# Two state-space heads rewritten: folded normalization, DMA borders, and a convolution shared by three engines

## The chip, the cores and the metric

The kernel runs on one core of a Trainium2 chip. The core has a matrix engine (TensorE, PE in the profile), a vector engine (VectorE, DVE), an activation engine (ScalarE, ACT), a general engine (GpSimd, POOL) and a queue engine (SyncE, SP), which here only issues DMAs. Each engine works through its own instruction stream in order, and semaphores tie the streams together. The metric is device time in microseconds for one launch, and lower is better. The kernel before takes 1484.87 us, the median of three runs (1484.46 to 1489.54).

## The reference, cut to what matters

Two layers run one after the other on an image of 64 x 64 tokens with 96 channels. All data is fp32. Both layers have this form (the second has its own weights for each of four scan directions, snake orders instead of plain ones, and a true recurrence):

```
xz = norm(x) @ in_proj_w               # 96 -> 384: x_val (192 channels) and z (192)
x_val = silu(depthwise_conv3x3(x_val) + conv_b)
y = sum over 4 scan directions of selective_scan(x_val) + D * x_val
out = (layernorm(y) * silu(z)) @ out_proj_w
```

In the kernel, each layer's input is first normalized over groups of three channels and all tokens; one mean and one variance per group give a factor `rs` and an offset `shift = -mean * rs` for each of the 96 channels. The output of layer 0, added to its input, is the input of layer 1.

## The kernel before

**Layout.** The input of a layer lies as `xT`, 96 channels by 4096 tokens. The 192 inner channels are three blocks `b` of 64 channels. A block's tile has 128 partitions: the lower 64 hold its channels for the first 512 tokens of every chunk of 1024, the upper 64 for the second 512. There are four chunks `c` (`NCH`), and a 512-token piece is 8 image rows (`SR`) of 64 (`HW`). `u[b]` is the result of the convolution, `y[b]` the running sum of the scans, both 128 x 2048.

**Order of a layer.** `head` makes `u`, starts `y` as `D * u`, and writes `silu(z)` to DRAM (`szd`). Then come the scans: in layer 0 `near_scans`, which works only on the ends of the sequences, and a branch that is skipped when it covers everything; in layer 1 `scans`, the long stage from some 256 us to the end. Then a tail applies the layer norm, the gate from `szd` and the output projection.

**The head.** Statistics (L1270 to L1282) end in `shift`. Eight instructions, four on VectorE and four on ScalarE (L1288, L1290), write the normalized input `xn`. `project(b, c)` is two products of 64 columns, one for each half of the partitions, and a ScalarE copy of the result into `pad[b]`, a tile of four chunks of 10 x 66 with room for a border on each side. `borders(b)` computes the row above and the row below each 8-row piece again, by four small products (L1315) and four ScalarE copies (L1319).

The convolution has nine taps. On VectorE, `conv` sums over two chunks at a time (128 x 1052 elements an instruction, L1373 for the first tap and L1375 for the other eight) into an SBUF tile `acc`; it does both pairs of blocks 0 and 1, and the last chunk of block 2. TensorE does three chunks of block 2 (`conv_by_products`, L1350): each tap is a product with a diagonal matrix `diag`, summed in PSUM. ScalarE applies SiLU (L1340) and starts `y` (L1250, `start_y`). Last, `gate(b, c)` takes two products of 64 columns (L1327) and a SiLU (L1332), and a DMA of 128 partitions to `szd` (L1333). PSUM in the head: three rooms for `z`, three for projections and products, two for borders.

**Order of work.** In the head before, engine calls are made on `nc.vector`, `nc.scalar` and so on: the framework's scheduler is free to reorder what is independent, and it moves weight loads of layer 1 into idle places of the SP queue. Calls made on `pe`, `act`, `dve`, `pool` and `sp` keep the order in which they are written on their engine; `near_scans` and `scans` use these. Helpers of this kind give one line number to all they record (L261 in `near_scans`, L738 in `scans`), so tiles' names must tell operations apart.

**What waits for the head.** In layer 0, `near_scans` begins with TensorE products of `u[T]` (tile `nu`), which ScalarE and VectorE copy out (`nus`), and then `npj`, `npd` and so on; `npd` needs the tile `nxd`, set to one by a GpSimd memset (L284). In layer 1, `scans` begins with TensorE's `pj`, twelve instructions over the last chunk of all three `u`; then ScalarE's `xd`, TensorE's `pd` and a softplus on ScalarE and VectorE; then DMAs of `su` to `du` issued by GpSimd.

Of the kernel before, what the change touches and what calls it, by code (L numbers as in the profile page):

```python
# [9 lines left out]
F32 = mybir.dt.float32  # L10
BF16 = mybir.dt.bfloat16
AF = mybir.ActivationFunctionType
ALU = mybir.AluOpType
# [4 lines left out]
HW = 64  # L18
L = HW * HW
# [25 lines left out]
def two_ss2d_layers(  # L45
# [1203 lines left out]
    def start_y(mul, ds, T, s=slice(0, L // 2)):  # L1249
        mul(y[T][:, s], u[T][:, s], ds[:, T : T + 1])  # L1250

    def head(l, xT, w):

        ipw_s, v, ds = w["ipw"], w["v"], w["ds"]
        with ExitStack() as sc:
            cv = sc.enter_context(tc.tile_pool(name=f"cv{l}", bufs=1, reuse_waits="tile"))
            cw = sc.enter_context(tc.tile_pool(name=f"cw{l}", bufs=3, reuse_waits="tile"))
            cvp = sc.enter_context(tc.tile_pool(name=f"cvp{l}", bufs=2, space=PSUM, reuse_waits="tile"))

            pad = [cv.tile([128, NCH, SR + 2, HW + 2], F32, name=f"pad{l}_{b}") for b in range(3)]  # L1260
            for t in pad:
                nc.gpsimd.memset(t[:, :, :, 0:1], 0.0)
                nc.gpsimd.memset(t[:, :, :, HW + 1 : HW + 2], 0.0)
                nc.gpsimd.memset(t[HALF[0], 0, 0, 1 : HW + 1], 0.0)
                nc.gpsimd.memset(t[HALF[1], NCH - 1, SR + 1, 1 : HW + 1], 0.0)


            gst = cv.tile([DM, 7], F32, name=f"gst{l}")
            gm, rs, shift = gst[:, 2:3], gst[:, 5:6], gst[:, 6:7]
            nc.vector.bn_aggr(gst[:, 0:2], w["st"].rearrange("p a b -> p (a b)"))  # L1270
            pm = cvp.tile([DM, 1], F32, tag="z", name=f"pm{l}", bufs=3)
            nc.tensor.matmul(pm, gav, gst[:, 0:1], start=True, stop=True)
            nc.vector.tensor_copy(gm, pm)
            nc.vector.tensor_sub(gst[:, 3:4], gst[:, 0:1], gm)
            nc.vector.tensor_mul(gst[:, 3:4], gst[:, 3:4], gst[:, 3:4])
            nc.vector.tensor_add(gst[:, 4:5], gst[:, 3:4], gst[:, 1:2])
            pv = cvp.tile([DM, 1], F32, tag="z", name=f"pv{l}", bufs=3)
            nc.tensor.matmul(pv, gav, gst[:, 4:5], start=True, stop=True)
            nc.scalar.activation(rs, pv, AF.Ln, bias=eps5[0:DM])
            nc.scalar.activation(rs, rs, AF.Exp, scale=-0.5)  # L1280

            nc.vector.scalar_tensor_tensor(shift, gm, -1.0, rs, ALU.mult, ALU.mult)  # L1282

            xn = cv.tile([DM, L], F32, name=f"xn{l}")
            for g in range(8):
                s = slice(g * 512, (g + 1) * 512)
                if g % 2 == 0:
                    nc.vector.tensor_scalar(xn[:, s], xT[:, s], gm, rs, ALU.subtract, ALU.mult)  # L1288
                else:
                    nc.scalar.activation(xn[:, s], xT[:, s], AF.Identity, bias=shift, scale=rs)  # L1290
            xr = xn.rearrange("p (r w) -> p r w", w=HW)

            def project(b, c):
                ps = cvp.tile([128, HT], F32, tag="in", name=f"in{l}_{b}_{c}", bufs=3)
                for h, half in enumerate(HALF):
                    g = 2 * c + h
                    nc.tensor.matmul(
                        ps[half], ipw_s[:, 64 * b : 64 * b + 64], xn[:, g * 512 : (g + 1) * 512],
                        start=True, stop=True,
                    )  # L1300
                nc.scalar.copy(
                    pad[b][:, c, 1 : SR + 1, 1 : HW + 1], ps.rearrange("p (r w) -> p r w", w=HW)
                )

            def borders(b):

                ps = cvp.tile([128, 2, NCH, HW], F32, tag="ed", name=f"ed{l}_{b}")
                lhs = ipw_s[:, 64 * b : 64 * b + 64]
                for h, half in enumerate(HALF):
                    for below in range(2):  # L1310

                        row = [SR * (2 * c + h + below) - 1 + below for c in range(NCH)]
                        cs = [c for c in range(NCH) if 0 <= row[c] < HW]
                        s = slice(cs[0], cs[-1] + 1)
                        nc.tensor.matmul(  # L1315
                            ps[half, below, s], lhs, xr[:, row[cs[0]] : row[cs[-1]] + 1 : 2 * SR],
                            start=True, stop=True,
                        )
                        nc.scalar.copy(  # L1319
                            pad[b][half, s, (SR + 1) * below, 1 : HW + 1], ps[half, below, s]  # L1320
                        )

            def gate(b, c):
                ps = cvp.tile([128, HT], F32, tag="z", name=f"z{l}_{b}_{c}", bufs=3)
                for h, half in enumerate(HALF):
                    g = 2 * c + h
                    nc.tensor.matmul(  # L1327
                        ps[half], ipw_s[:, DI + 64 * b : DI + 64 * b + 64],
                        xn[:, g * 512 : (g + 1) * 512], start=True, stop=True,
                    )  # L1330
                sz = cw.tile([128, HT], F32, tag="sz", name=f"sz{l}_{b}_{c}")
                nc.scalar.activation(sz, ps, AF.Silu)  # L1332
                nc.sync.dma_start(out=szd[l][b, :, HT * c : HT * (c + 1)], in_=sz)  # L1333

            taps = [(i, j) for i in range(3) for j in range(3)]

            W2 = HW + 2

            def finish(b, cut, of):
                nc.scalar.activation(  # L1340
                    u[b][:, cut].rearrange("p (c r w) -> p c r w", r=SR, w=HW), of, AF.Silu,
                    bias=v[:, b, V_CB : V_CB + 1],
                )
                start_y(nc.scalar.mul, ds, b, cut)

            def conv_by_products(b, c):

                ps = cvp.tile([128, HT], F32, tag="in", name=f"cp{l}_{b}_{c}", bufs=3)
                for k, (i, j) in enumerate(taps):
                    nc.tensor.matmul(  # L1350
                        ps.rearrange("p (r w) -> p r w", w=HW), diag[:, k, :],
                        pad[b][:, c, i : i + SR, j : j + HW],
                        start=(k == 0), stop=(k == len(taps) - 1),
                    )
                finish(
                    b, slice(HT * c, HT * (c + 1)), ps.rearrange("p (c r w) -> p c r w", c=1, w=HW)
                )

            def conv(b, s):


                n = s.stop - s.start
                room = cw.tile([128, 2, SR, W2], F32, tag="acc", name=f"acc{l}_{b}_{s.start}")
                room = room[:, 0:n]
                acc = room.rearrange("p c r w -> p c (r w)")[:, :, 0 : SR * W2 - 2]
                for k, (i, j) in enumerate(taps):
                    o = i * W2 + j
                    src = pad[b].rearrange("p c r w -> p c (r w)")[
                        :, s, o : o + SR * W2 - 2
                    ]  # L1370
                    wk = v[:, b, V_CW + k : V_CW + k + 1]
                    if k == 0:
                        nc.vector.tensor_scalar_mul(acc, src, wk)  # L1373
                    else:
                        nc.vector.scalar_tensor_tensor(acc, src, wk, acc, ALU.mult, ALU.add)  # L1375
                finish(b, slice(HT * s.start, HT * s.stop), room[:, :, :, 0:HW])

            for b in (0, 1, 2):
                project(b, 0)
                project(b, 1)  # L1380
                borders(b)
            for b in (2, 0, 1):
                project(b, 2)
                project(b, 3)
            diag = cv.tile([128, len(taps), 128], F32, name=f"diag{l}")
            for k in range(len(taps)):
                nc.scalar.mul(diag[:, k, :], ident, v[:, 2, V_CW + k : V_CW + k + 1])
            conv(0, slice(0, 2))
            for c in range(NCH - 1):
                conv_by_products(2, c)  # L1390
            for b, c in ((1, 0), (0, 2), (1, 2)):
                conv(b, slice(c, c + 2))
            conv(2, slice(NCH - 1, NCH))
            for b in range(3):
                for c in range(NCH):
                    gate(b, c)

    def tail(l, w, xT):

# [349 lines left out]
```

## Time and profile before

| | us |
|---|---|
| median of three runs | 1484.87 |
| the profiled execution, own time | 1483.21 |
| its span, first to last instruction | 1481.1 |
| head of layer 0: `shift` ready, to first copy of `nus` | 21.32 to 80.36 |
| head of layer 1: `shift` ready, to end of `pj` | 196.47 to 261.61 |
| convolution on VectorE, layer 1, first tap to last | 206.36 to 255.25 |

Busy shares over the span: PE 83%, DVE 91%, ACT 82%, POOL 75%. The span is nearly all `scans` (from 290 us on). In the two heads POOL is idle but for a few memsets.

How to read the rows: a row of the timeline has a start, a length, the engine, the line and operation, the output and input tiles, partitions x elements, a count, and in brackets the idle time before with the instruction that ended it. A group's row ends in busy time and mean ns of one. In the table of stretches each engine has its busy time and number of instructions; the number after POOL's is the clock that TensorE was granted (1.00 is full), then the DMA share and GB/s. TensorE's fp32 products are two instructions each in this profile.

### The profile page before, as it was taken

The page shows a single profiled execution, that of the slowest core. Times are in us where ns is not written, and L with a number is a line of the kernel's source. Part 1 is how long each engine was busy: PE and PEld are TensorE (multiplying, and loading weights), DVE is VectorE, ACT ScalarE, POOL GpSimd, SP SyncE. Part 2 cuts the span into 40 slices and gives each one's busy share as a digit, 9 for nine tenths or more (in the row PEclk, how much of TensorE's full clock was granted, in tenths as well). Part 3 has the DMA queues.
Part 4 walks back from the last instruction along what each step waited for, and adds up shares of the span by engine and source line. Part 5 has one row for each costly group of instructions (what it writes and reads, how often), then busy time and mean ns, then how long its engine had stood idle before and what let it go on. Part 6 is the DMA issues. An engine that isn't in the chain of part 4 may idle for free.

```text
span 1481.1 us, 17275 instructions
## 1 busy us (share of the span) xinstructions
PE 1229.0 (83%) x5091; PEld 487.2 (33%) x5091; DVE 1345.5 (91%) x945; ACT 1212.4 (82%) x2500; POOL 1109.5 (75%) x603
## 2 busy tenths in 40 slices
PE   6955888698788888879888888888889898887898
PEld 3333333233232323233333333333333332322333
DVE  5957679589999999999999999999998999999996
ACT  6564345689999989998999999999997989897873
POOL 1003000379999998989898989898989898989895
PEclk9965889589999999999999999999998999999999
DMA  4230612515262626262626262626262626262634
GB/s 113 74 94 6 154 28 86 129 33 129 70 144 59 148 67 148 58 155 57 145 57 145 59 143 59 143 59 143 60 144 57 143 59 153 61 145 69 144 87 127
DMA packets 79793, 146.30 MB, mean 99 GB/s; under 512 B 27676, under 2 KB 30940, under 8 KB 79596
## 3 DMA queue, kind: packets, MB, share of 16 engines
q1 hardware_dynamic: 78012, 142.58, 39.7%
q0 software_dynamic: 576, 1.57, 0.4%
q10 hardware_dynamic: 1104, 0.98, 0.2%
q8 instruction: 41, 0.67, 0.2%
q14 instruction: 60, 0.49, 0.1%
HBM read 80.85 MB, written 12.13 MB: 63 GB/s over the span
## 4 chain that ended last, share of the span: by engine, by line
DVE 27%; issue 20%; ACT 12%; PE 11%; POOL 10%; DMA 6%; SPq 3%; DVEq 0%; POOLq 0%; ACTq 0%
DVE h L738 15%; DVE b L738 7%; POOL hc L738 7%; ACT a L738 4%; ACT bT L738 3%; DMA cb<-C 3%; PE pj L738 3%; SPq L738 3%; PE ys L738 3%; DVE acc L1375 3%; PE b L738 2%; DMA xT<-xs 2%; POOL sp L738 1%; POOL ln L738 1%; DMA du<-su 1%
## 5 line engine op out<-in xcount | busy, mean ns | idle before, releaser
L738 POOL TENSOR_TENSOR hc<-h,cb 128x1024 f32<-128x1024 f32 x384 | 902.8, 2372 | 92.9 <-DVE h L738 40.1
L738 DVE TENSOR_TENSOR_SCAN h<-a,carry,b 128x1024 f32<-128x1024 f32 x288 | 664.5, 2337 | 23.6 <-PE b L738 2.6
L738 ACT ACTIVATE a<-dt,am 128x1024 f32<-128x1024 f32 x384 | 437.9, 1141 | 56.7 <-DVE h L738 50.6
L738 PE MATMUL ys<-hc,fold 128*64 128x512 f32 x1536 | 430.3, 640 | 0.1
L738 ACT ACTIVATE bT<-duT,BT 128x192 f32<-128x192 f32 x1012 | 386.6, 445 | 2.2
L738 PE MATMUL b<-ident,bT 128*128 128x128 f32 x1536 | 224.1, 289 | 28.9 <-DVE h L738 19.4
L738 DVE TENSOR_TENSOR b<-b,du 128x1024 f32<-128x1024 f32 x192 | 232.0, 1208 | 8.6 <-PE b L738 8.4
L738 PEld LDWEIGHTS b<-ident,bT 128*128 128x128 f32 x1536 | 176.5, 146 | 153.5 <-DVE h L738 90.1
L738 DVE TENSOR_TENSOR_SCAN h<-a,b 128x1024 f32<-128x1024 f32 x96 | 216.4, 2278 | 11.2 <-PE b L738 2.4
L738 PE MATMUL b<-B,selh 96*128 96x512 bf16 x384 | 117.6, 388 | 125.9 <-DVE h L738 125.5
L738 PEld LDWEIGHTS ys<-hc,fold 128*64 128x64 f32 x1536 | 77.7, 138 | 140.0 <-issue 106.3
L738 PEld LDWEIGHTS <-selh 96*128 96x128 bf16 x384 | 25.7, 98 | 255.3 <-DVE h L738 204.9
L738 PE MATMUL pj<-u,xw 64*124 64x512 f32 x192 | 100.6, 671 | 4.3 <-ACT sz L1332 2.0
L1375 DVE SCALAR_TENSOR_TENSOR acc<-pad,v,acc 128x1052 f32<-128x1052 f32 (+1 forms) x80 | 91.4, 1200 | 0.7
L738 POOL DMA_DIRECT2D du<-su x12 | 6.4, 538 | 83.2 <-ACT am L235 80.8
L261 POOL MEMSET nna<- 128x4 f32 (+1 forms) x9 | 1.0, 117 | 86.1 <-ACT nna L261 86.1
L738 ACT CAST B<-pj 96x512 bf16<-96x512 f32 (+2 forms) x96 | 54.9, 575 | 5.1 <-PE pj L738 5.1
L738 POOL TENSOR_TENSOR sp<-sp,ln 128x512 f32<-128x512 f32 x45 | 57.7, 1283 | 0.2
L738 POOL TENSOR_TENSOR ln<-ln,w 128x512 f32<-128x512 f32 x45 | 57.8, 1285 | 0.0
L738 POOL TENSOR_TENSOR su<-sp,u 128x512 f32<-128x512 f32 x45 | 57.6, 1281 | 0.0
L738 PE MATMUL ys<-y,ident 128*128 128x512 f32 (+1 forms) x120 | 57.2, 577 | 0.0
L738 PEld LDWEIGHTS pj<-u,xw 64*124 64x124 f32 x192 | 35.2, 199 | 65.8 <-issue 48.7
(189 smaller groups left out, 1224.0 us busy)
## 6 DMA issues: line engine op xcount, KB each, us to landing
cb<-C SPq DMA_DIRECT2D x256, 256.0 KB
dt<-sp SPq DMA_DIRECT2D x192, 128.0 KB
du<-su SPq DMA_DIRECT2D x180, 128.0 KB
szd<-sz SPq DMA_DIRECT2D x24, 256.0 KB
szt<-szd SPq DMA_DIRECT2D x24, 256.0 KB
xT<-xs SPq DMA_DIRECT2D x8, 384.0 KB
xs<-xT SPq DMA_DIRECT2D x1, 1536.0 KB
xs<-xT SPq DMA_DIRECT2D x8, 192.0 KB
```

What stands on the lines that cost most here:

```text
L261: return lambda *args, **more: tc.keep_in_program_order(op(*args, **more))
L738: return lambda *args, **more: tc.keep_in_program_order(op(*args, **more))
L1375: nc.vector.scalar_tensor_tensor(acc, src, wk, acc, ALU.mult, ALU.add)
```

## The change

It rewrites `head` for both layers.

- The normalization is folded into the projection: VectorE scales the weights by `rs` (`ws`, three instructions), nine products with one moving column (`offset`) give the constant term of every output channel, and one copy makes them a bias tile. `xn` and its eight instructions go; all products read `xT`. The copies into `pad` and the gates' SiLUs add the bias.
- The border rows are no longer computed: after the four copies of a block, four DMAs on SP move rows between the halves of `pad` (64 partitions, rows of 64 elements).
- The convolution is split over more engines. VectorE does three pairs (block 0 both, block 1 the first), with its sums in PSUM (`accs`, five banks). TensorE does three chunks of block 2 as before. Three chunks (block 2's last, block 1's last two) are made by ScalarE, which multiplies each tap into a tile, and GpSimd, which adds the tiles up.
- For blocks 0 and 1, a gate product has all 128 columns and one 512-token piece (`gate01`), and its result goes to `szd` by two DMAs of 64 partitions. Block 2 stays as it was (`gate2`).
- `start_y` moves from ScalarE to GpSimd, six instructions of 128 x 1024, after the convolution.
- All of it is put into a list with times and issued in the order of these times, on the ordered engines. PSUM has three rooms for all other results. The ring of `sz` tiles has four buffers instead of three.

```diff
+            for k in range(9):
+                act.mul(diag[:, k, :], ident, v[:, 2, V_CW + k : V_CW + k + 1])
 ...
+            accs = cvp.tile([128, 5 * HT], F32, name=f"accs{l}")
+            small = accs[:, 4 * SR * W2 : 4 * SR * W2 + 8]
 ...
-            xn = cv.tile([DM, L], F32, name=f"xn{l}")
-            for g in range(8):
-                s = slice(g * 512, (g + 1) * 512)
-                if g % 2 == 0:
-                    nc.vector.tensor_scalar(xn[:, s], xT[:, s], gm, rs, ALU.subtract, ALU.mult)
-                else:
-                    nc.scalar.activation(xn[:, s], xT[:, s], AF.Identity, bias=shift, scale=rs)
+            for cut in (slice(0, 64), slice(64, DI), slice(DI, 2 * DI)):
+                dve.tensor_scalar_mul(ws[:, cut], ipw_s[:, cut], rs)
+            def offset(to, of, n):
+                pe.matmul(
+                    small[to, 2 + n : 3 + n], ipw_s[:, of : of + to.stop - to.start], shift,
+                    start=True, stop=True,
+                )
+            for half in HALF:
+                offset(half, 0, 0)
+            for n in (1, 2):
+                for half in HALF:
+                    offset(half, 64 * n, n)
+            offset(slice(0, 128), DI, 3)
+            for half in HALF:
+                offset(half, DI + 128, 4)
+            dve.tensor_copy(bias, small[:, 2:7])
+            def room(name):
+                return cvp.tile([128, HT], F32, tag="in", name=name, bufs=3)
+            def padded(b, c):
+                act.activation(
+                    pad[b][:, c, 1 : SR + 1, 1 : HW + 1],
+                    live.pop(("in", b, c)).rearrange("p (r w) -> p r w", w=HW),
+                    AF.Identity, bias=bias[:, b : b + 1],
+                )
             def borders(b):
-                ps = cvp.tile([128, 2, NCH, HW], F32, tag="ed", name=f"ed{l}_{b}")
 ...
+                t, n = pad[b], NCH - 1
+                row = slice(1, HW + 1)
+                h0, h1 = HALF
+                sp.dma_start(out=t[h1, :, 0, row], in_=t[h0, :, SR, row])
+                sp.dma_start(out=t[h0, 1:, 0, row], in_=t[h1, :n, SR, row])
+                sp.dma_start(out=t[h0, :, SR + 1, row], in_=t[h1, :, 1, row])
+                sp.dma_start(out=t[h1, :n, SR + 1, row], in_=t[h0, 1:, 1, row])
+            def gate01(g):
+                ps = live["z", g] = room(f"z{l}_{g}")
+                pe.matmul(
+                    ps, ws[:, DI : DI + 128], xT[:, g * 512 : (g + 1) * 512], start=True, stop=True
+                )
+            def gated01(g):
+                c, h = divmod(g, 2)
+                sz = cw.tile([128, HT], F32, tag="sz", name=f"sz{l}_{g}")
+                act.activation(sz, live.pop(("z", g)), AF.Silu, bias=bias[:, 3:4])
+                for b, half in enumerate(HALF):
+                    sp.dma_start(
+                        out=szd[l][b, HALF[h], HT * c : HT * (c + 1)], in_=sz[half]
+                    )
 ...
+            taps = [(i, j) for i in (1, 0, 2) for j in range(3)]
 ...
+            def tap_dve(n, b, c, k):
+                i, j = taps[k]
+                o = i * W2 + j
+                acc = accs[:, 2 * SR * W2 * (n % 2) :][:, 0 : 2 * SR * W2]
+                live["acc", b, c] = acc.rearrange("p (c r w) -> p c r w", r=SR, w=W2)
+                acc = acc.rearrange("p (c t) -> p c t", c=2)[:, :, 0 : SR * W2 - 2]
 ...
+            def tap_act(b, c, k):
+                t = cw.tile(
+                    [128, HT], F32, tag="tap" if k else "sum", name=f"tap{l}_{b}_{c}_{k}",
+                    bufs=3 if k else 2,
+                )
+                live["tap" if k else "sum", b, c, k] = t
+                act.mul(t.rearrange("p (r w) -> p r w", w=HW), source(b, c, *taps[k]), weight(b, *taps[k]))
+            def tap_pool(b, c, k):
+                acc = live["sum", b, c, 0]
+                pool.tensor_add(acc, acc, live.pop(("tap", b, c, k)))
+            t = 0.0
+            for b, order in ((0, (2, 3, 1, 0)), (2, (3, 2, 1, 0)), (1, (3, 2, 1, 0))):
+                for c in order:
+                    at(t, project, b, c)
+                    at(t + 0.95, padded, b, c)
+                    t += 0.9
+                at(t + 1.0, borders, b)
+            for c in range(3):
+                for k in range(9):
+                    at(t + 0.9 * k, tap_pe, 2, c, k)
+                t += 8.1
+                at(t + 0.1, silu, 2, slice(HT * c, HT * (c + 1)), partial(whole, ("cp", c)))
+            for g in range(8):
+                at(t, gate01, g)
+                at(t + 0.5, gated01, g)
+                t += 0.5
+            for c in range(NCH):
+                at(t, gate2, c)
+                at(t + 0.9, gated2, c)
+                t += 0.9
+            t = 2.6
+            for n, (b, c) in enumerate(((0, 2), (0, 0), (1, 0))):
+                for k in range(9):
+                    at(t, tap_dve, n, b, c, k)
+                    t += 1.3
 ...
+            t = 7.4
+            for b, c in ((2, 3), (1, 3), (1, 2)):
+                for k in range(9):
+                    at(t - 1.5, tap_act, b, c, k)
+                    if k:
+                        at(t, tap_pool, b, c, k)
+                        t += 1.3
 ...
+            for n, (b, c) in enumerate(((2, 2), (0, 2), (1, 2), (2, 0), (0, 0), (1, 0))):
+                at(
+                    t + 1.5 + 2.5 * n, start_y, pool.tensor_scalar_mul, ds, b,
+                    slice(HT * c, HT * (c + 2)),
+                )
+            for _, _, step in sorted(steps, key=lambda at: at[:2]):
+                step()
```

## The prediction

> **What bounds the kernel now.** I read the page first, then the chain of waits, then the timeline of each engine in the two heads, since the change touches nothing else. The chain from 193 to 264 us belongs to layer 1:
>
> ```profile
> 196.47 0.47 DVE xn L1288
> ...
> 209.16 12.31 DVE acc L1375 x11
> ...
> 254.49 0.78 DVE acc L1375
> 255.29 0.73 ACT u L1340
> 256.06 5.55 PE pj L738 x8
> ```
>
> VectorE's convolution holds the path from 206.36 to 255.3; then a SiLU, then `pj`. The chain does not reach back into layer 0, so there I read the timeline:
>
> ```profile
> 62.33 9.66 PE L1327 MATMUL z<-xn,ipw 96*64 96x512 f32 x44
> 72.41 1.08 PE L1327 MATMUL z<-xn,ipw 96*64 96x512 f32 x4 [0.42 <-ACT sz L1332]
> 76.98 5.43 PE L261 MATMUL nu<-u,wide 128*128 128x192 f32 x24 [3.49 <-ACT sz L1332]
> 78.97 0.72 ACT L1340 ACTIVATE u<-acc,v 128x512 f32<-128x512 f32 x1 [2.05 <-DVE acc L1375]
> 80.36 0.46 ACT L261 COPY nus<-nu 128x384 f32<-128x384 f32 x1
> ```
>
> TensorE's gates and their SiLUs end at 76.9, VectorE's convolution at 78.9. So TensorE is late by nearly as much as VectorE, and taking work off VectorE alone gains little. I count from `shift` ready (21.32 and 196.47): layer 0's first `nus` copy is at 59.0, layer 1's `pj` ends at 65.1. What the change does to these two moments is the forecast.
>
> **TensorE's path, part by part.** Rows for its prices, from the timeline and from the stretches (the last number but two is the clock):
>
> ```profile
> 20.15 0.45 PE L1278 MATMUL pv<-gst,gav 96*96 96x1 f32 x2 [0.91 <-DVE gst L1276]
> 21.83 5.06 PE L1297 MATMUL in<-xn,ipw 96*64 96x512 f32 x12 [1.23 <-DVE xn L1288]
> 38.95 23.45 PE L1350 MATMUL cp<-pad,diag 128*128 128x512 f32 x54
> ```
> ```profile
> 25.00:26.00 1.00, 1.00 (x5) 0.46 (x3) 0.00 (x0) 0.07 (x1) 0.79 (x2) 0.50 0.04 0
> 26.00:27.00 1.00, 1.00 (x7) 0.55 (x4) 0.00 (x0) 0.52 (x1) 1.00 (x2) 0.98 0.16 12
> ```
>
> *Normalization.* Eight `xn` instructions go; the first product needed only one of them, so it started at 0.5. Now nine one-column products (18 instructions) stand before it: 0.17 each by `in`'s weight loads (four in 0.68) to 0.22 by `pv` (two in 0.45), 3.1 to 4.0; I take 3.5. The three scalings of weights lie beside them on VectorE. This costs 3.0.
>
> *Projections.* A pair of halves is four instructions: 1.7 at half clock (twelve in 5.06), 0.88 at full clock (44 `z` in 9.66). The clock rose 4.2 us after the first large product in layer 0 and 6.3 after it in layer 1; I take 5, so three pairs at 1.7 and nine at 0.88: the eighth pair, the last of block 2, ends at 3.5 + 5.1 + 4.4 = 13.0 and the twelfth at 16.5.
>
> *Borders.* Twelve small products and twelve of ScalarE's copies in each layer go (0.32 and 0.37). In their place come four DMAs a block. The nearest row is `nS`, 64 partitions from SBUF to SBUF: 0.55 to issue, and its second half was waited for until 1.8 after. Block 2's copies end at about 15 (taps stand between them), so its upper rows land at 15 + 1.2 + 1.9 = 18.1. ScalarE meets this wait: the fourth tap of chunk 3 needs those rows, and behind it on its queue stand three copies of block 1. These free the rooms that TensorE's first `cp` product needs. So `cp` starts not at 16.5 but at 18.1 + 1.4 = 19.5; before, 17.6 and 18.8. With its 23.5 unchanged it ends at 43.0.
>
> *Gates.* A product of 128 columns costs two instructions of 0.434 (54 `cp` in 23.45), 0.87; two of 64 columns cost four of 0.22, 0.88. Wider products therefore save nothing here: 12 x 0.87 = 10.5 as before (at best, if columns set the price, 0.44 each, 3.4 less). But the DMAs grow from 12 to 20. A 128-partition issue took 0.32; for 64 partitions I take 0.55 of `nS` (bounds 0.32 and 0.61). The first `sz` is ready at 44.5; sixteen half issues end at 53.3, the last lands at 55.2, and with four buffers the last SiLU waits for it: 55.8. ScalarE has a queue of other SiLUs here; I add 1.0 (0 to 3): 56.8. TensorE's last gate waits for a room and ends near 54.5.
>
> **What lies beside it.** *VectorE:* 24 taps at 1.23 (fourteen in 17.23) and three first taps at about 1.2 (0.76 in SBUF; a sum in PSUM, `nb` of 1024, took 1.23): 33, from 7.7 with some 4 of waits for borders and SiLUs to 45, hidden by TensorE. *ScalarE:* 12 copies and 12 gates at 0.6, 27 taps at 0.72, nine SiLUs 7.6, a table 1.3: 43 in 57, hidden but for the queue above. *GpSimd:* 24 adds at 1.28 are 31; most wait for 18.1, so they end near 50. *SP in layer 0* issues weight loads without a gap until 57; each border DMA waits for one at most (0.65) if the scheduler places it when ready, as it did with `xs`, which started at 17.69 right after its last copy.
>
> *`start_y`* leaves ScalarE (0.72 and 1.15 each) for GpSimd, at 50, six times d. Rows on both sides:
>
> ```profile
> L738 POOL TENSOR_SCALAR bT<-duT,BT 128x192 f32<-128x192 f32 x4 | 3.0, 756 | 5.4 <-DVE duT L738 5.4
> L294 POOL COPY picked<-i 32x1024 f32<-32x1024 f32 x1 | 1.0, 1027 | 0.0
> ```
>
> d is 1.03 by the copy of as many elements, 4.0 by 756 ns for 192. I take 1.3, nearer to the copy, which also has one input. Behind these six stand, in layer 0, the memset of `nxd` (0.73; it must wait for the last read of `xT`), needed by `npd` at 67.3 - 2.2 = 65.1; and in layer 1 the `du` DMAs at 74.0 - 5.8 = 68.2. Both stay hidden while d is under 2.4 and 3.0.
>
> The Trainium skill's "GPSIMD Engine Reference", section 3.1, gives 1.03 cycles an element for bodies of this kind, by my estimate 0.9 us for 1024, against 3.9 ns an element in the row; its "SBUF - State Buffer", section "Who interferes with whom", would explain the row, as VectorE ran scalings of its own (403 ns) beside it and blocks GpSimd in its two-port modes. By the page `start_y` is over by 56; by the row it is not over before 74.
>
> A rule against the change is in "DMA: Bandwidth & Descriptors", Specifications: below 512 bytes a write is a read-modify-write, and border rows have 256. The rows of `nS` have 1536, so no run here shows it. If it doubled the 1.9 to land, each layer would lose 1.9 and the sum below would be 4.2.
>
> **The sum.** Layer 0: `nus` at 56.8 instead of 59.0, gain 2.2. Layer 1: `pj` starts at 54.5 and TensorE has not rested, so twelve at 0.434 end at 59.7 instead of 65.1, gain 5.4, and 0.4 for `pd` at full clock. Together 8.0. The profiled execution took 1483.21, so 1475.2; it is 1.66 below the median, which gives 1476.9. Faster or slower by over 0.5% is 7.4 us, about what a measurement of this kernel can tell from no change.
>
> **Rivals.**
> 1. *The same (chance 0.36).* The head only trades one late stage for another: half clock until 6.8 after the first large product (+1.5), half issues at 0.61 (+1), landings or ScalarE's queue 1 longer (+1). A gain of 8.0 less 3.5 in each layer is 1.0: 1483.9. For it: TensorE's work in the stage is nearly what it was.
> 2. *Faster still (0.12).* Half issues at 0.32 (-3.5), no queue on ScalarE (-1), `nu` at full clock where 77 to 80 was at 0.50 (up to -3): some 3.5 more a layer, 15 in all, 1470. Against it: the wait for borders stays.
> 3. *Slower, GpSimd becomes the bound (0.09).* With d = 4.0 `start_y` ends at 74. Layer 0 waits in `npd`: 74 + 0.7 - 65.1 = 9.6. Layer 1 waits in `du`: 5.8. With the 8.0 that is 7.4 slower, 1492.3. It eats the whole gain from d = 3.4.
> 4. *Slower, SP's order (0.09).* If the border DMAs of layer 0 stand behind all 44 early loads, which end at 57.1 (35.8 after `shift`), block 2's rows land at 35.8 + 3.3 + 1.9 = 41.0 instead of 18.1, and the layer ends 22.9 later: 1499.8. Each load ahead costs 0.63; 13 take the gain, 25 make it slower. Against it: `xs` was placed without delay.
>
> **How the numbers follow.** The forecast itself, a gain of 7.4 to 12, has 0.34. Faster is 0.34 + 0.12, same 0.36, slower 0.18. The range runs from 1467, a little beyond rival 2, to 1494, which takes in rival 3; left out are rival 4 and the tails, under 0.2.
>
> **What would show it.** Right: the first large product 3 to 4 after `shift`; ScalarE idle on a DMA of `pad` near 15 to 18; `cp` beginning near 19.5; VectorE's last tap before the gates end; `pj` with no wait for VectorE. Wrong: `cp` beginning over 25 in layer 0 (SP), `npd` or `du` waiting for GpSimd, 128-column products well under 0.8, or VectorE's taps in PSUM over 1.5, which would make it the bound again.

## The result

The changed kernel takes 1483.0 us, the median of 13 runs (1478.38 to 1491.32), against 1484.0 for the kernel before on the same chips: a ratio of 0.9993, 95% interval 0.9973 to 1.0013. That is no change; a gain of 8.0 had been forecast. The profiled execution of the changed kernel took 1485.29, span 1483.5, at a mean granted clock of 0.932 (before 0.928).

The total hides two differences of opposite sign. Both are counted from `shift` ready, 21.67 in layer 0 and 202.53 in layer 1:

| | before | predicted | after |
|---|---|---|---|
| layer 0: `cp` on TensorE | 17.6 to 41.1 | 19.5 to 43.0 | 17.6 to 42.5 |
| layer 0: last `sz` ends | 55.6 | 55.8 to 56.8 | 62.7 |
| layer 0: first `nus` copy | 59.0 | 56.8 | 64.1 |
| layer 1: `pj` ends | 65.1 | 59.7 | 59.8 |
| layer 1: first `wl` | 67.8 | 62.0 | 61.7 |

Layer 1 gained 6.1 up to the first `wl`, as forecast (5.8). Layer 0 lost 5.0 instead of gaining 2.2. Another 0.3 was lost ahead of layer 0's `shift`, 0.7 between the first `nus` and layer 1's `shift`, and 0.3 behind `wl`, so that the first `a` of the long scan stage starts at 277.49 us instead of 277.28.

**Layer 0: where the 5.0 went.** First SP's timeline of the changed kernel (the rows between are weight loads, all alike):

```profile
25.58 0.60 SPq L224 DMA_DIRECT2D ab<-in_alb_dram  x1
30.33 7.26 SPq L261 DMA_DIRECT2D pad<-pad  x8
37.64 0.60 SPq L1716 DMA_DIRECT2D ipw<-in_ipw_dram  x1
...
41.63 2.58 SPq L261 DMA_DIRECT2D pad<-pad  x4
...
69.99 0.60 SPq L224 DMA_DIRECT2D ab<-in_alb_dram  x1
70.69 13.99 SPq L261 DMA_DIRECT2D szd<-sz  x20
```

The same rows of the kernel before, for comparison:

```profile
56.51 0.60 SPq L224 DMA_DIRECT2D ab<-in_alb_dram  x1
64.39 12.88 SPq L1333 DMA_DIRECT2D szd<-sz  x12
```

No border DMA waited for more than one load (block 1's four, by 0.7). Instead SP stood from 26.2 to 30.3 with a border DMA at the head of its queue, because ScalarE had not yet made the rows, and again for 1.0 before block 2's. Of the twelve issues, eleven took 0.59 to 0.64 and one 1.59. The end of the weight loads moved by 13.5 us, from 57.1 to 70.6, and the first `szd` write came behind the last load. The first `sz` tile had been ready since 67.4. What follows from it on ScalarE and TensorE:

```profile
67.89 1.84 ACT L261 ACTIVATE sz<-z,bias 128x512 f32<-128x512 f32 x3
73.80 0.69 ACT L261 ACTIVATE sz<-z,bias 128x512 f32<-128x512 f32 x1 [4.07 <-DMA szd<-sz]
74.54 9.01 PE L261 MATMUL z<-xT,ws 96*128 96x512 f32 x18 [3.07 <-ACT sz L261]
85.75 0.48 ACT L261 COPY nus<-nu 128x384 f32<-128x384 f32 x1 [1.41 <-PE nu L261]
```

All four `sz` buffers are full; the fifth SiLU waits 4.07 for the first buffer to be written out, TensorE waits 3.07 for a room, and 18 of its 32 gate instructions are still to come.

**Layer 1: where the gain came from.** The chain of waits of the changed kernel there:

```profile
211.22 0.68 SPq L261
211.96 3.80 DMA pad<-pad
215.88 1.33 DVE accs L261
...
238.89 1.11 ACT u L261
240.00 1.23 ACT tap L261 x2
241.30 1.29 POOL tap L261
...
248.56 0.49 SPq L261
249.10 2.39 DMA szd<-sz
251.59 0.69 ACT sz L261
...
257.49 1.08 PE z L261 x4
258.56 3.75 PE pj L738 x12
```

VectorE's convolution no longer runs to the end of the stage; it leaves the chain at 238.9, and ScalarE's taps and SiLUs, GpSimd's adds, `szd` and TensorE's gates carry the rest. `pj` follows the last gate without a pause: all twelve instructions take 3.75, where the last eight alone took 5.55 before.

The stretches of the same layer show a cost inside this (the last number but two is the granted clock):

```profile
218.00:219.00 1.00, 0.00 (x0) 0.00 (x0) 0.96 (x2) 0.28 (x1) 0.00 (x0) 1.00 0.46 97
219.00:220.00 1.00, 0.00 (x0) 0.00 (x0) 0.91 (x2) 1.00 (x3) 0.42 (x1) 0.93 0.25 52
220.00:221.00 1.00, 0.84 (x1) 0.50 (x2) 1.00 (x1) 1.00 (x3) 0.92 (x2) 0.50 0.00 0
...
222.00:223.00 1.00, 1.00 (x3) 0.48 (x2) 0.96 (x2) 1.00 (x3) 0.68 (x2) 0.50 0.00 0
223.00:224.00 1.00, 1.00 (x4) 0.46 (x3) 1.00 (x1) 0.98 (x2) 0.92 (x2) 0.86 0.48 103
```

TensorE idles 2.28 us, since ScalarE waits for border rows, and then its clock is at 0.50 for some 3 us: `cp` takes 24.96 instead of 23.45.

The groups of the changed kernel that the prediction had priced (busy us, mean ns of one | idle time before):

```profile
L261 DVE SCALAR_TENSOR_TENSOR accs<-pad,v,accs 128x1052 f32<-128x1052 f32 x48 | 63.3, 1319 | 12.7 <-DMA pad<-pad 6.3 <-ACT u L261 4.7
L261 POOL TENSOR_TENSOR tap<-tap,tap 128x512 f32<-128x512 f32 x48 | 61.0, 1273 | 47.8 <-ACT tap L261 45.0
L261 POOL TENSOR_SCALAR y<-u,ds 128x1024 f32<-128x1024 f32 x12 | 33.9, 2843 | 1.2 <-ACT u L261 1.2
```

`start_y` costs GpSimd 2.84 us an instruction, not 1.3.

### The profile page after: what moved, and what is told of

Read it like the earlier page. It is cut to its first block, busy times and chain, and to the rows that moved or that the text cites. A ratio compares the mean times of both kernels' runs of the same rounds, so it can differ in the third digit from the quotient of the medians.

```text
span 1483.5 us, 17337 instructions
## 1 busy us (share of the span) xinstructions
PE 1222.3 (82%) x5047; PEld 480.5 (32%) x5047; DVE 1317.1 (89%) x909; ACT 1224.9 (83%) x2508; POOL 1205.4 (81%) x663
## 4 chain that ended last, share of the span: by engine, by line
DVE 30%; issue 23%; PE 10%; ACT 10%; POOL 7%; DMA 6%; SPq 2%; DVEq 0%; POOLq 0%; ACTq 0%
DVE h L738 19%; DVE b L738 8%; POOL hc L738 5%; ACT a L738 3%; PE ys L738 3%; ACT bT L738 2%; PE pj L738 2%; DMA cb<-C 2%; PE b L738 2%; SPq L738 2%; DVE accs L261 1%; DMA szt<-szd 1%; DMA xT<-xs 1%; DMA du<-su 1%; PE pd L738 1%
## 5 line engine op out<-in xcount | busy, mean ns | idle before, releaser
L738 DVE TENSOR_TENSOR_SCAN h<-a,carry,b 128x1024 f32<-128x1024 f32 x288 | 664.6, 2337 | 26.2 <-PE b L738 3.5
L738 PE MATMUL b<-ident,bT 128*128 128x128 f32 x1536 | 219.4, 286 | 26.4 <-DVE h L738 18.2
L261 POOL TENSOR_TENSOR tap<-tap,tap 128x512 f32<-128x512 f32 x48 | 61.0, 1273 | 47.8 <-ACT tap L261 45.0
L738 PE MATMUL pj<-u,xw 64*124 64x512 f32 x192 | 94.1, 635 | 1.9 <-DVE w L738 1.2
L261 DVE SCALAR_TENSOR_TENSOR accs<-pad,v,accs 128x1052 f32<-128x1052 f32 x48 | 63.3, 1319 | 12.7 <-DMA pad<-pad 6.3
L738 PE MATMUL ys<-y,ident 128*128 128x512 f32 (+1 forms) x120 | 61.2, 612 | 0.0
L738 POOL TENSOR_TENSOR sp<-sp,ln 128x512 f32<-128x512 f32 x45 | 57.8, 1284 | 0.2
L738 POOL TENSOR_TENSOR su<-sp,u 128x512 f32<-128x512 f32 x45 | 57.7, 1282 | 0.0
L261 POOL MEMSET pad<- 128x40 f32 (+1 forms) x24 | 2.7, 170 | 67.0 <-DVE g L1524 51.1
L738 PE MATMUL pd<-xd,dwb 29*64 29x512 f32 x192 | 55.0, 646 | 0.0
```

The costliest lines, as they stand in the source:

```text
L261: return lambda *args, **more: tc.keep_in_program_order(op(*args, **more))
L738: return lambda *args, **more: tc.keep_in_program_order(op(*args, **more))
```

## The experiments

The main theory, called T below: the new head loses 5.0 in layer 0 by SP's order, and gains 5 to 6 in layer 1. The kernels ran on chips where the kernel before took 1485.3 to 1488.3, so ratios are compared, and beside them two moments of each head, whose spread between profiles is about 1 us, and the start of the first `a`, which sums up all before the scan stage. (That sum also carries the start of layer 0's `shift`, 20.5 to 21.7, and the stretch between the heads, which no edit touches: from the first `nw` to layer 1's `shift` it took 103.7 to 106.6.) Run e10, of which there is one execution only, has its own paragraph.

| run | `nus`, layer 0 | `pj` ends, layer 1 | first `a` | ratio to before, 95% |
|---|---|---|---|---|
| before | 59.0 | 65.1 | 277.3 | |
| after | 64.1 | 59.8 | 277.5 | 0.9993 (0.9973 to 1.0013) |
| e1_new0_old1 | 63.3 | 65.2 | 281.4 | 1.0020 (0.9997 to 1.0042) |
| e2_old0_new1 | 60.3 | 59.5 | 272.9 | 0.9988 (0.9963 to 1.0013) |
| e3_sz12 | 56.5 | 57.8 | 271.2 | 0.9956 (0.9933 to 0.9979) |
| e4_bord_pool | 58.5 | 59.9 | 272.1 | 0.9992 (0.9969 to 1.0015) |
| e5_sz12_ydve | 57.4 | 58.1 | 265.2 | 0.9918 (0.9898 to 0.9937) |
| e6_ydve | 64.2 | 59.8 | 276.7 | 0.9999 (0.9976 to 1.0022) |
| e7_narrow | 60.6 | 57.7 | 268.6 | 0.9961 (0.9938 to 0.9984) |
| e8_old_sz12 | 58.7 | 65.3 | 276.2 | 1.0001 (0.9980 to 1.0021) |
| e9_order | 56.7 | 58.2 | 264.4 | 0.9931 (0.9902 to 0.9961) |
| e11_order4 | 61.5 | 60.0 | 271.9 | 0.9971 (0.9951 to 0.9991) |
| e12_best_narrow | 55.9 | 57.6 | 264.0 | 0.9898 (0.9867 to 0.9929) |

**One layer at a time.**

```diff
-        head(l, xT, w)
+        (head_old if l else head)(l, xT, w)     # e1: new head in layer 0 only
+        (head if l else head_old)(l, xT, w)     # e2: new head in layer 1 only
```

> The new head in layer 0 only, layer 1 as before. Theory (T): the new head loses 5.0 us in layer 0 (first nus copy 64.1 after shift instead of 59.0) and gains 5.3 to 6.1 in layer 1, and the two cancel. T expects nus at 64.1, layer 1's pj end at 65.1 as before, and 5.0 slower than before: 1484.0 + 5.0 = 1489.0. Rival (S): the long scan stage swallows or adds what the heads do, so that neither head moves the end; it expects 1484 within 1.5.

> The new head in layer 1 only, layer 0 as before. T expects first nus at 59.0, pj end at 59.8, and a gain of 5.3 to 6.1: 1478.3. S expects 1484 within 1.5.

The heads behaved as T says: 63.3 with the old 65.2, and 60.3 with the new 59.5. At the first `a` the one is 4.1 later than before and the other 4.4 earlier. In the total, e1 is 0.2% slower (3.0 us, interval -0.4 to 6.2) and e2 0.1% faster (1.8 us, -1.9 to 5.5). Both lie on the side that T names, but neither excludes zero, so by time alone the rival of a scan stage that swallows everything was not excluded here; e5 does that below.

**More buffers.** The ring of `sz` tiles is made twelve deep, so that no SiLU waits for a write.

```diff
-                sz = cw.tile([128, HT], F32, tag="sz", name=f"sz{l}_{g}")
+                sz = cw.tile([128, HT], F32, tag="sz", name=f"sz{l}_{g}", bufs=12)
```

> The new head in both layers with twelve sz buffers instead of four, so that no SiLU of the gates waits for a szd DMA. T (the szd DMAs of layer 0 stand on SP behind weight loads which the border DMAs pushed from 57 to 70.6 us, and ScalarE waits 4.1 us and TensorE 3.1 us for buffers): the gates follow TensorE, ten of 0.9 from 66.9, so nus at 56.5 instead of 64.1 (7.6 less) and pj end at 58.3 instead of 59.8; 1483.0 - 9.1 = 1473.9. Rival (Q): ScalarE's queue (SiLUs that wait for VectorE's and GpSimd's sums, at 69.7 and 70.9) sets the end of the gates, buffers or not: nus at 63 to 64, 1482 to 1483.

`nus` at 56.5 and `pj` at 57.8, as T had it. ScalarE's queue is not what held the gates. But the first `a` came only 6.3 earlier than in the changed kernel, not 9.1, and 1.1 of the 6.3 lies ahead of layer 0's `shift`. The timeline of layer 0 in this run shows who came next:

```profile
69.28 13.72 SPq L261 DMA_DIRECT2D szd<-sz  x20
69.20 16.96 POOL L261 TENSOR_SCALAR y<-u,ds 128x1024 f32<-128x1024 f32 x6
86.22 0.73 POOL L284 MEMSET nxd<- 32x768 f32 x1
86.98 0.48 ACT L261 COPY nxd<-npj 124x384 f32<-124x384 f32 x1 [2.84 <-POOL nxd L284]
90.69 0.49 ACT L261 ACTIVATE nw<-npd 128x384 f32<-128x384 f32 x1 [2.87 <-PE npd L261]
```

SP's first write is as late as in the changed kernel, and nobody waits for it. Now GpSimd's six `start_y` hold the memset of `nxd`, ScalarE waits 2.84 for that, and the first `nw` comes at 90.69, where the kernel before has it at 90.72. Layer 0's whole gain is given back here. This is the wait in `npd` of which the prediction's rival 3 spoke.

**Border DMAs on another queue.**

```diff
-                sp.dma_start(out=t[h1, :, 0, row], in_=t[h0, :, SR, row])     # and three more
+                pool.dma_start(out=t[h1, :, 0, row], in_=t[h0, :, SR, row])
```

> The new head in both layers, its border DMAs issued by GpSimd instead of SP; all else as it was, four sz buffers. T: SP's weight loads end at 57 again, szd is written as it comes from 67.5 on, and layer 0 behaves like layer 1: nus at 60.3 instead of 64.1, pj end 59.8 as it was; 1483.0 - 3.8 = 1479.2. The price that could hide it: GpSimd's adds wait behind the DMAs of block 1, some 3 us, and the DMAs may land later. Rival (H): it is the twenty szd issues of 0.7 that are long, whatever stands before them: nus stays at 63 to 64, 1483.

SP's timeline in this run:

```profile
55.46 0.60 SPq L224 DMA_DIRECT2D ab<-in_alb_dram  x1
67.05 13.10 SPq L261 DMA_DIRECT2D szd<-sz  x20
```

With the waiting border DMAs off SP, the loads end at 56.1, `szd` follows the first `sz` directly, and the wait of 4.07 is gone; `nus` comes 5.5 earlier than in the changed kernel. Of this 1.8 lies ahead of the gates, since `cp` started 0.3 earlier and ran at full clock in this profile; from the first gate product to `nus` it took 18.0 instead of 21.7. e1's layer 0 also had `cp` at 23.42, with the border DMAs on SP, and its `nus` is 4.7 later than here. The edit takes the border DMAs out of SP's order and changes nothing else, so that order costs layer 0 some 4 to 5, and the length of the twenty issues (13.1 here too) does not. The first `a` gained 5.4 on the changed kernel, but the timed ratio does not show it (0.9992, some 1 us with an interval of 3.4 either way); why stays open.

**GpSimd's share.** `start_y` goes to VectorE, which idles from 48 us after `shift` on; in e5 with twelve buffers, in e6 with four.

```diff
-                    t + 1.5 + 2.5 * n, start_y, pool.tensor_scalar_mul, ds, b,
+                    t + 1.5 + 2.5 * n, start_y, dve.tensor_scalar_mul, ds, b,
```

> Twelve sz buffers, and start_y on VectorE instead of GpSimd. In the run with twelve buffers alone, the first layer's head was 2.6 us shorter than before at nus but npd's results came at the same 90.7 us: ScalarE waited 2.84 us for GpSimd's memset of nxd, which stood behind six start_y of 2.83. Theory (G): once the szd wait is gone GpSimd is the next bound, 2.8 in layer 0 and about 1.2 in layer 1 (from wl to the first a took 14.1 instead of 13.0). G expects no wait for nxd, nw at 87.8, wl to a in 12.9, and 4.0 less than with twelve buffers alone: about 1478.5 where the kernel before takes 1488.3. Rival (N): the next bound is somewhere else (SP's szd issues to 83, TensorE at half clock), and nw stays near 90: no more than 1 less than with twelve buffers alone.

> start_y on VectorE, but four sz buffers as in the changed kernel. G: with the late szd the six start_y of 2.83 were hidden, so nothing moves: nus at 64 after shift in layer 0, npd 8.1 after nus, pj end 59.8, the same time as the changed kernel within 1 us. Rival (P): GpSimd's start_y slows other work by its memory traffic or holds the du DMAs even now; then it gains 2 to 4.

Layer 0 in e5:

```profile
69.69 2.42 DVE L261 TENSOR_SCALAR y<-u,ds 128x1024 f32<-128x1024 f32 x2
73.32 2.74 DVE L261 TENSOR_SCALAR y<-u,ds 128x1024 f32<-128x1024 f32 x4 [1.20 <-ACT u L261]
85.74 0.48 ACT L261 COPY nxd<-npj 124x384 f32<-124x384 f32 x1 [0.45 <-PE npj L261]
88.40 0.49 ACT L261 ACTIVATE nw<-npd 128x384 f32<-128x384 f32 x1 [1.83 <-PE npd L261]
```

The wait for `nxd` is gone, `nw` follows `nus` as closely as before, and in layer 1 the first `a` comes 12.9 after the first `wl` instead of the 14.1 of e3. With four buffers (e6) the same edit moves nothing. So `start_y` on GpSimd was hidden in the changed kernel only because SP was later still. e5 reaches the first `a` 12.0 earlier than the kernel before; 9.6 of this lie in the two heads and what follows them (1.76 from `shift` to `nw` in layer 0, 7.88 from `shift` to `a` in layer 1), the rest elsewhere. Its time is 12.2 us below (9.4 to 15.2): a gain in the heads does reach the end.

**The shape of the gates.** In e7 the gates of blocks 0 and 1 go back to products of 64 columns with one DMA of 128 partitions each, twelve issues instead of twenty.

```diff
-                        ps[half], ws[:, DI + 128 : 2 * DI], xT[:, g * 512 : (g + 1) * 512],
+                        ps[half], ws[:, DI + 64 * b : DI + 64 * b + 64], xT[:, g * 512 : (g + 1) * 512],
 ...
-                at(t, gate01, g)
-                at(t + 0.5, gated01, g)
+                at(t, gate2, g % 4, g // 4)
+                at(t + 0.5, gated2, g % 4, g // 4)
```

> The gates of blocks 0 and 1 as before: products of 64 columns, one szd DMA of 128 partitions for each (12 instead of 20), 18 instructions of offsets become 24; four sz buffers, all else as in the changed kernel. T (SP is late because of the weight loads; the half DMAs add little): layer 0 keeps the 4.1 us wait, TensorE's nine last gates are the same 9.0, nus at 62.5 to 64; in layer 1 the six waits of 0.3 to 0.8 for szd go, pj end 58.3. Together 2 to 3 less. Rival (H): the twenty issues of 0.7 are what makes the gates long; then layer 0 gains as much as layer 1 or more: nus at 59 to 60, and 5 less. Rival (W): wider products do save TensorE time and this loses 3 in each layer.

It gained more than T said: `nus` 3.5 and `pj` 2.1 earlier. Most of this lies ahead of the gates. In this profile `cp` took 23.42 in both layers and began 0.7 and 1.1 earlier. From the first gate product to `nus`, and to the end of `pj`, it needed 20.3 and 17.8 us where the changed kernel needed 21.7 and 17.3. By this count the gates gave 1.4 in layer 0 and lost 0.4 in layer 1. Against e1's layer 0, whose `cp` also took 23.42 with the wide gates, `nus` is 2.7 earlier. So fewer issues are worth 1.4 to 2.7 where SP is late: H has part of layer 0 right, but not its 5 or more, the fifth SiLU still waited 3.54 for `szd`, and W falls. Why `cp` ran at full clock is the question of e12.

**The kernel before with twelve buffers.**

```diff
-                sz = cw.tile([128, HT], F32, tag="sz", name=f"sz{l}_{b}_{c}")
+                sz = cw.tile([128, HT], F32, tag="sz", name=f"sz{l}_{b}_{c}", bufs=12)
```

> The kernel before, with twelve sz buffers instead of three. It tells whether the buffers alone are worth what they gave the new head. Theory: in the kernel before the ends of both heads wait for VectorE's convolution (57.6 and 58.8 after shift), and the gates end ahead of it, so nothing is gained: nus 59 to 60, pj end 65.1, the time of the kernel before within 1 us. Rival: the buffers are the whole gain, and it gains 5.

As expected, nothing (1.0001): the old heads wait for VectorE.

**The wait for border rows.** Block 2 is projected first, so that its rows are there when ScalarE needs them; in e9 on top of e5, in e11 on the changed kernel.

```diff
-            for b, order in ((0, (2, 3, 1, 0)), (2, (3, 2, 1, 0)), (1, (3, 2, 1, 0))):
+            for b, order in ((2, (3, 2, 1, 0)), (0, (2, 3, 1, 0)), (1, (3, 2, 1, 0))):
 ...
-            t = 2.6
+            t = 6.2
```

> As the run with twelve sz buffers and start_y on VectorE, and block 2 is projected first (blocks 2, 0, 1 instead of 0, 2, 1; VectorE's taps listed 3.6 later), so that ScalarE's fourth tap finds block 2's border rows landed. Theory (B): the wait for border rows costs TensorE 2.3 us idle in each layer, after which the granted clock falls to 0.50 and the first products cost 1.5 more. B expects cp to start at 15.5 to 16 after shift instead of 17.7 to 18.2 and to take 23.45 instead of 25.0, VectorE's last tap at 50, nus at 55 instead of 57.4, pj end at 56 instead of 58.1, 4 to 4.5 less in all: about 11 + 4.5 = 15.5 below the kernel before. Rival (V): VectorE, which starts 3 to 5 later, becomes the bound; its last tap comes at 52 or later and nothing is gained.

> The changed kernel with nothing but the block order of the projections changed (2, 0, 1; four sz buffers, start_y on GpSimd). T (layer 0 is held by SP, whose loads end at 70 whatever TensorE does) and B together expect that cp ends 3 to 4 earlier in both layers, that layer 1 gains 2 (pj end 57.8) and that layer 0 gains under 1 (nus 63 to 64). Rival (Q): ScalarE's and TensorE's own queues set layer 0's gates; then it gains as much as layer 1, nus at 61 to 62.

The wait went: in e9 `cp` starts at 15.2, straight after the projections, and takes 23.45 in both layers. Yet `nus` gained 0.7 and `pj` nothing, and the ratio is that of e5 within the intervals. TensorE waits later instead:

```profile
64.23 10.70 PE L261 MATMUL z<-xT,ws 96*128 96x512 f32 x28 [3.29 <-ACT u L261]
```

The room for its third gate is freed by a SiLU of `cp`, which stands in ScalarE's queue behind taps that wait for GpSimd and a SiLU that waits for VectorE (whose last tap now comes at 51.1, 2.1 later than in e5). B was right on the wait and wrong on its worth; V was right that nothing is gained, with a last tap 0.9 earlier than the 52 it named. In e11 layer 0 gained 2.6 and layer 1 nothing. Q had the 61.5 of layer 0 but expected as much in layer 1, and T had neither: SP's own wait for border rows was shorter too, its loads ended at 69.1 instead of 70.6, and the fifth SiLU still waited 3.68 for `szd`.

**VectorE's sums in SBUF.**

```diff
-                acc = accs[:, 2 * SR * W2 * (n % 2) :][:, 0 : 2 * SR * W2]
+                if k == 0:
+                    live["room"] = cw.tile([128, 2 * SR * W2], F32, tag="acc", name=f"acc{l}_{n}", bufs=2)
+                acc = live["room"]
```

> The changed kernel with VectorE's sums in SBUF tiles instead of PSUM; all else as it was. Theory: a tap costs 1.32 to 1.35 in PSUM, and 1.23 in SBUF as before; VectorE's last tap comes 1.5 to 3 earlier (45 to 46.5 after shift), and it is hidden: nus at 64 and pj end at 59.8 stay within 0.5. Rival: beside GpSimd's adds a tap in SBUF costs more, 1.35 or over.

The rival was right, far beyond its number. The groups of this run:

```profile
L261 DVE SCALAR_TENSOR_TENSOR acc<-pad,v,acc 128x1052 f32<-128x1052 f32 x48 | 98.5, 2052 | 8.7 <-DMA pad<-pad 6.9
L261 POOL TENSOR_TENSOR tap<-tap,tap 128x512 f32<-128x512 f32 x48 | 98.4, 2053 | 41.4 <-ACT tap L261 38.3
```

VectorE's taps went from 1.32 to 2.05 us and GpSimd's adds from 1.27 to 2.05; VectorE's last tap came at 63.5 instead of 48.1, `pj` ended 13.7 later, and the one run took 1513.5. Only the place of the sums was changed, so it is the sums in PSUM that let the two engines work side by side here.

**The last combination.** Twelve buffers, `start_y` on VectorE, and the gates of e7.

> Twelve sz buffers, start_y on VectorE, and the gates of blocks 0 and 1 by 64 columns with whole DMAs. Theory (T): with twelve buffers nobody waits for szd, so the shape of the gates is worth nothing: nus at 57 and pj end at 58 after shift as with the wider gates, 11 to 12 below the kernel before. Rival (C): the narrow gates' head keeps TensorE's full clock in the convolution (23.4 for cp where most runs show 25.0), through its 24 offset products instead of 18; then both heads are 2 shorter, nus at 55 and pj end at 56, some 15 below the kernel before. Rival (W): the wide product saves TensorE time, and this loses 1 or more in each layer.

TensorE in layer 0:

```profile
38.74 24.98 PE L261 MATMUL cp<-pad,diag 128*128 128x512 f32 x54 [2.28 <-ACT pad L261]
63.66 1.94 PE L261 MATMUL z<-xT,ws 96*64 96x512 f32 x8
66.03 8.92 PE L261 MATMUL z<-xT,ws 96*64 96x512 f32 x40 [0.44 <-ACT u L261]
```

`cp` took 24.98 here, and 25.07 in layer 1, so the 24 offset products do not keep the clock up: C falls, and what gave e7 its full clock is not known. Forty instructions of 64 columns took 8.92, and for the same ten gates 28 instructions, wide ones and block 2's, took 9.05 in e3's layer 1: the wide product saves nothing. e12 has the lowest median of all, 1472.8, a ratio of 0.9898; e5 is not separated from it.

## Why the prediction was wrong

**The step that failed is SP's sentence in layer 0.** It asked only how long a border DMA waits for the loads in front of it ("each border DMA waits for one at most"), and for that it was right: only block 1's waited, 0.7 for one load. It did not ask what stands behind a border DMA that itself waits. Rival 4 named SP's order, but again as border DMAs behind loads. The trace has the reverse: 49 loads behind the first eight border DMAs, 43 of them behind all twelve, 13.5 us, and `szd` behind the loads. The term for the gates in layer 0 took "the first `sz` is ready at 44.5" as the start of the sixteen half issues; it was ready at 45.7, and they started at 49.0. `nus` came 7.3 later than the 56.8 of the prediction. SP's order is 4 to 5 of this (e4 against the changed kernel and against e1); e3, with twelve buffers that make any wait for `szd` harmless, regained 7.6.

**The ring of four was right as a mechanism** and too small as a term: in layer 1, without loads, the last `sz` ended at 58.9 where 55.8 to 56.8 was written, and twelve buffers gave 2.0 there.

**Rival 1, "the same", had the total by luck.** Its 1483.9 is near the 1483.0 measured, but it let each layer fall 3.5 short of the forecast, for reasons on TensorE, in the issues and on ScalarE. Layer 1 did not fall short, and layer 0 fell 7.3 short, mostly by SP's order, which was rival 4's subject.

**Layer 1 held.** `pj` ended at 59.8 for 59.7, though by two misses that cancel: the last gate came 1.5 later than 54.5, and `pj` took 3.80 instead of 12 x 0.434 = 5.2. `pd` at full clock gave more than the 0.4 (3.53 instead of 6.12 before).

**Smaller terms.** Offsets: 1.63 for 18 instructions, not 3.5; nine products of one column cost 0.09 an instruction when they follow each other, not the 0.17 to 0.22 taken. Projections: the last ended at 15.3 for 16.5. `cp` therefore started at 17.6 for 19.5, right after a wait for border rows (2.25 on ScalarE) that the prediction had placed well; but `cp` took 24.94 for 23.5, with the clock at 0.50 behind the pause, so it ended at 42.5 for 43.0. Gates: "wider products save nothing" held. VectorE's taps: 1.32 for 1.23, which had come from one stretch; over all of the kernel before the mean was 1.308, so PSUM costs next to nothing here. Its last tap came at 48 for 45 and was hidden. GpSimd's adds ended at 49.2 for 50.

**`start_y`: d was 2.84, and 1.3 had been taken**, from a copy as the nearest row. It lies above the 2.4 that the prediction gave as the limit in layer 0 and just below 3.0 in layer 1. It stayed hidden only because layer 0 was late anyway (e6), and came out as rival 3 once that was mended (e3 against e5). The bounds, 1.03 and 4.0, held it.

**GpSimd beside VectorE, and the border rows.** In layer 0 VectorE was idle but for two copies of 0.56 while GpSimd's six `start_y` ran at 2.83, so their price is not VectorE's doing. The Trainium skill's "GPSIMD Engine Reference", section 3.1, which would make them 0.9 us by my estimate, disagrees with the 2.84 of this trace, and the measurement decides. Its "SBUF - State Buffer", section "Who interferes with whom", says that a VectorE instruction with two inputs in SBUF contends with GpSimd's reads and that one with a single SBUF input, outside the two-port modes, does not; e10 against the changed kernel is just this pair, 2.05 against 1.32, and it agrees. That page's full exclusion is not quite seen: a tap and an add of 1.32 and 1.27 in strict turn would take 2.59, and where both ran almost without a gap in layer 0 of e10 a tap took 2.23 (eight in 17.86). The read-modify-write that the prediction cited from "DMA: Bandwidth & Descriptors" for border rows did not double their landing where it counted: ScalarE's wait for block 2's rows ended 1.5 to 1.6 after their issue in both layers, for the 1.9 taken. In e4, where the trace has landings, block 0's rows landed 2.1 to 4.0 after the start of their issue and the other blocks' 1.9 to 2.3; why block 0's took longer stays open.

## What to carry to other kernels

When a DMA is put on an in-order queue, price what stands behind it while it waits for its data, not only what stands in front: here waits of 4.1 and 1.0 us and twelve short issues moved the end of 49 weight loads by 13.5 us and, through them, the writes that free a ring of buffers. When a late stage is mended, look for the engine that its lateness had hidden: GpSimd's 17 us of `start_y` cost nothing until SP was out of the way. VectorE and GpSimd slowed each other to 2.05 us an instruction with VectorE's sums in SBUF and ran at 1.32 and 1.27 with them in PSUM, so where a running sum lives is worth a look before work is split between these two.

## What was not expected of the hardware

A TensorE pause of only 2.3 to 2.6 us was mostly followed by a stretch at a granted clock of 0.50, and whether it was varied: over the eighteen new heads with this pause, `cp` took 23.42 in five, with the clock at 1.00 throughout, and 24.8 to 26.5 in thirteen, which had the stretch at 0.50. GpSimd's scaling of 128 x 1024 fp32 elements takes 2.84 us, VectorE's 0.75 (four of them in e5, GpSimd at rest). VectorE's first one in e5, which began at 69.69 while GpSimd's last add ran until 70.90, took 1.76.
